# Turns for one pair of blocks, sums before the first layer, and one gate for the gathers of four units

## The chip, the cores and the metric

The kernel runs on one core of a Trainium2 chip. The metric is the device time of one launch in microseconds, the median of three runs. Engines are named as in the profile: PE is TensorE's matmuls, PEld its weight loads, DVE VectorE, ACT ScalarE, POOL GpSimd, SP SyncE.

## The reference, cut to what matters

One layer of a graph network over 6250 nodes of 256 features and 206250 edges, sorted by their target node `dst`:

```
h    = relu(layernorm(x))
e    = relu(raw @ W_e1.T + b_e1) @ W_e2.T + b_e2       # raw: 64 features of an edge
emb  = (e * (clip(edge_attr[:, 0], 0, 1) + 0.01)) @ W_le.T + b_le
msg  = relu(h[src] + emb)
aggr = segment_sum(msg, dst)
g    = (h + aggr) @ W_g1.T + b_g1
out  = x + relu(layernorm(g) * ln_g + ln_b) @ W_g2.T + b_g2
```

All of it is in float32.

## The kernel before, in words

Edges are cut into 403 blocks of 512 and these into 806 units of 256 (two tiles of 128 edges). W_e2 and W_le are multiplied once at the start, so an edge needs a first layer (64 to 256) and one product (256 to 256). Everything is unrolled, and the order on every engine is the order in which the program emits it (a hand-written schedule). The loop runs over units `u`; `now` is the unit in hand. What it emits for a unit:

- `edge_part(u)` (L317): four matmuls (L325, 128x128 weights, 256 columns) into one of seven PSUM banks, which go round in a ring (`BANKS`, class `Ring`); DVE adds the offset and writes `msg[u]` (L331), which frees the bank. In the trace each float32 matmul stands as two records.
- `turn_of(u // 4)`, if `u % 4 == TURN`. A pair `q` is two blocks, that is four units. A turn holds `first_layer(q + 2)` (L278: for each half `c` of the 256 outputs, one matmul for each of the two blocks, each on 64 rows, L292; then ACT and DVE apply bias and relu, L308 and L305, and free the four banks), the segment sums (`add_pairs`, L735, called as `sums`), and the load of the raw features of a later pair on SP's queue (`load_pair`, L273).
- `piece()`: a piece of the 0/1 matrices for the sums (L663, DVE).
- `whole(v)` (L677) for units that lie `lag` units behind: DVE multiplies `msg[v]` by the edge's polarity and adds the gathered row of `h` (L685, in place in `hg[v]`), ACT applies the relu (L690). `lag` falls from 18 to 1 in the course of the kernel, and is one more in the unit ahead of a turn.
- `due()` (L904): a step of the work on 128 finished nodes (two transposes L166 and L199, two products L181 and L212), four steps for each such block of nodes, kept out of the units that `QUIET` names.

The sums of a block (`add_up`, L692) are four matmuls (L703), one for each tile, each with a 0/1 matrix of 32 columns and into its own 32 partitions of the bank `pd`. `add_pairs` takes all pairs whose units `whole` has been through; the first of its matmuls for a pair waits for the newest of these units.

In the middle of the list (`by_two(q)`: 6 <= q < 196) every second turn does the work of two pairs: sums for two pairs, then two first layers, then two loads; the turns between are empty. At both ends each turn does one pair, first layer first.

The rows of `h` are fetched by POOL, two indirect DMAs to a unit (`gather`, L627, issued at L634), into 20 buffers `hg` (`HG`). `got` counts gathers, `summed` the pairs whose sums have been emitted; a gather may run at most 20 units ahead of these. `in_step` (L646), called as `paced` after every unit and after each half of a first layer, adds PE's planned time to `spent` (EDGE 1.754 for a unit, LAYER 0.9 for half a first layer; `add_up` adds SUMS 0.46 a block, `due` NODES 0.81 a step) and emits gathers as long as `(got - 8) * STEP` is below `spent + AFLOAT` (1.288 and 6.0). The first gather that a call emits waits for the matmul that was just emitted; the others follow it on POOL's queue. From unit 782 on, gathers are emitted without such a wait as far as the buffers go.

Of the kernel before, what the change touches and what calls it, by code (L numbers as in the profile page):

```python
# [36 lines left out]
NP = -(-NB // 2)  # L37
# [3 lines left out]
LEAD = 22  # L41
LEAST = 1
EDGE, LAYER, SUMS, NODES = 1.754, 0.9, 0.46, 0.81
STEP = 1.288
AFLOAT = 6.0
BANKS = 7
SHRINK = 44
RAW = 4
HG = 16 + RAW
FEW = 6  # L50
QUIET = (0, 1)
TURN = 1
# [21 lines left out]
def groups_of(w):  # L74
    return [g for g in range(NG) if w in windows_of(g)]
# [25 lines left out]
def gnn_kernel(ctx: ExitStack, tc: tile.TileContext, x, src_c, dst_c, dst_r, pol_c, raw_t, w_e1t, w_e2,  # L101
# [37 lines left out]
    def behind(ins, other):  # L139

        if other is not None:
            tc.add_manual_dep(ins.ins, other.ins.name, mybir.DependencyInfo(
                mybir.DependencyClass.Sync, mybir.DependencyReason.DATA), reason="one wait for several")
# [90 lines left out]
    NU = 2 * NB  # L234
    fast = ExitStack()
    fast.enter_context(tc.manual_schedule())
    with fast:
# [11 lines left out]

        banks = [psz.tile([P, 2, D], F32, name=f"pz{i}") for i in range(BANKS)]  # L250

        class Ring:
# [4 lines left out]
            def __call__(self):  # L257
                self.taken += 1
                return banks[self.taken % BANKS]

# [6 lines left out]
            def old(self):  # L267
                n = self.taken - BANKS
                return self.readers.get(n), self.writers.get(n)
# [3 lines left out]
        def load_pair(q):  # L273
            if q < NP:
                raw[q] = ld.tile([P, 512], F32, name="raw")
                nc.sync.dma_start(out=raw[q], in_=raw_t[q])

        def first_layer(q):  # L278

            bs = [b for b in (2 * q, 2 * q + 1) if b < NB]  # L280
            if not bs:
                return
            for b in bs:
                e1[b] = e1_p.tile([P, 2, 512], F32, name="e1")
            pe, z = {}, {}
            for c in range(2):
                olds = []
                for s, b in enumerate(bs):
                    pe[s, c] = ps().rearrange("p a b -> p (a b)")
                    olds.append(ps.old())  # L290
                for s, b in enumerate(bs):
                    z[c] = nc.tensor.matmul(pe[s, c], we1_s[s * F:(s + 1) * F, c * P:(c + 1) * P],  # L292
                                            raw[q][s * F:(s + 1) * F, :], start=True, stop=True)
                    ps.wrote(z[c], len(bs) - 1 - s)
                    reader, writer = olds[s]
                    if reader is not None and writer is not None:
                        tc.declare_no_dep(z[c].ins, writer.ins, reason="the bank's reader has waited for it")
                    if s == 0:
                        for reader, _ in olds[1:]:
                            behind(z[c], reader)  # L300
                paced(LAYER, z[c])
            for c in range(2):
                for s, b in enumerate(bs):
                    if s == c == 1:
                        a = nc.vector.tensor_scalar(e1[b][:, c, :], pe[s, c], be1_s[:, c:c + 1], 0.0, op0=ALU.add,  # L305
                                                    op1=ALU.max)
                    else:
                        a = nc.scalar.activation(e1[b][:, c, :], pe[s, c], AF.Relu, bias=be1_s[:, c:c + 1])  # L308
                    behind(a, z[c])
                    ps.read(a, len(bs) * (1 - c) + len(bs) - 1 - s)  # L310
            raw.pop(q)
# [23 lines left out]

        last_z = None
        sums = lambda last: None
        paced = lambda us, behind: None

        def by_two(q):  # L340
            return FEW <= q < NP - FEW

        def turn_of(q):


            if not by_two(q):
                if q + 2 < NP:
                    first_layer(q + 2)
                sums(q == NP - 1)
                load_pair(q + 4)  # L350
            elif q % 2 == 0:
                sums(False)
                first_layer(q + 2)
                first_layer(q + 3)
                load_pair(q + 4)
                load_pair(q + 5)

        def forward(u):

            edge_part(u)  # L360
            if u % 4 == TURN:
                turn_of(u // 4)
# [44 lines left out]
        with tc.tile_pool(name="p1", bufs=4) as p1, tc.tile_pool(name="p1x", bufs=11) as p1x:  # L407
# [76 lines left out]
            for k in range(len(parts) + 1):  # L484
# [21 lines left out]
                for _ in range((k > 0) + (k > 2 and k % 3 > 0)):  # L506
                    u = next(units, None)
# [37 lines left out]
        def rows_of_edges():  # L545
            nc.vector.tensor_tensor(
                rel[:, :full].rearrange("p (g k j) -> p g k j", k=L, j=S),
                dst_f[:, :full].rearrange("p (g k j) -> p g k j", k=L, j=S),
                base_b[:, :NF, :].rearrange("p g (o j) -> p g o j", o=1).to_broadcast([P, NF, L, S]), ALU.subtract)
            nc.vector.tensor_tensor(rel[:, full:], dst_f[:, full:], base_b[:, NF, :], ALU.subtract)  # L550
# [63 lines left out]
        with tc.tile_pool(name="hg", bufs=HG - RAW) as hg_p, tc.tile_pool(name="ms", bufs=4) as ms_p, \  # L614
# [5 lines left out]
            got = 2 * RAW  # L620
# [3 lines left out]
            summed = 0  # L624
            spent = 0.0

            def gather(behind=None):  # L627

                nonlocal got
                u, i = divmod(got, 2)  # L630
                got += 1
                if i == 0:
                    hg[u] = (hx_p if u % HG < RAW else hg_p).tile([P, 2, D], F32, name="hg")
                g = nc.gpsimd.indirect_dma_start(  # L634
                    out=hg[u][:, i, :], out_offset=None, in_=hb_d,
                    in_offset=bass.IndirectOffsetOnAxis(ap=src_s[:, 2 * u + i:2 * u + i + 1], axis=0))
                if behind is not None:
                    tc.add_manual_dep(g.ins, behind.ins.name, mybir.DependencyInfo(
                        mybir.DependencyClass.Sync, mybir.DependencyReason.DATA), reason="gathers in step with PE")

            def gathers(last):

                while got < 2 * min(NU, last):
                    gather()

            def in_step(us, behind):  # L646

                nonlocal spent
                spent += us
                while (got - 2 * RAW) * STEP < spent + AFLOAT and got < 2 * min(NU, 4 * summed + HG):  # L650
                    gather(behind)
                    behind = None

            def select(g):

                return [(g, lambda k=k: rows_of_block(g, k)) for k in range(len(blocks_of(g)))]
# [11 lines left out]
            def piece():  # L668

                due_now = [s for s in steps if s[0] <= now][:1]  # L670
                if due_now:
                    steps.remove(due_now[0])
                    due_now[0][1]()
                elif rest:
                    rest.popleft()[1]()
# [81 lines left out]
            now = 0  # L757
# [146 lines left out]
            def due():  # L904

                nonlocal spent
                fns = todo.pop(now, deque())
                if fns and not (by_two(now // 4) and now % 8 in QUIET):
                    spent += NODES
                    fns.popleft()()  # L910
                if fns:
                    todo.setdefault(now + 1, deque()).extendleft(reversed(fns))

            gathers(RAW + 1)
            sums = add_pairs
            paced = in_step
            def strips():
                rows_of_edges()
                rest.extend(select(0) + select(1))
# [4 lines left out]
            now = LEAD  # L924
# [7 lines left out]
            for u in range(LEAD, NU):  # L932
                now = u
                forward(u)

                if u >= NU - 24:
                    gathers(4 * summed + HG)

                piece()
                lag = max(LEAST, LEAD - RAW - u // SHRINK) + (by_two(u // 4) and (u + 1) % 8 == TURN)  # L940
                ready_for = min(u + 1 - lag, 5 * (u + 1 - LEAD) // 4)
                while made < ready_for:
                    gathers(made + 1)
                    whole(made)
                    made += 1
                due()
                for fn in moves.pop(now, []):
                    fn()
                if len(rest) > 6:
                    piece()  # L950
                if u == NU - 24:
                    for w in range(NW):
                        if groups_of(w)[-1] == NG - 1:
                            late[w] = node_work(w, True)
                if u == LEAD + 60:
                    flag = nc.values_load(bad_i[0:1, 0:1], min_val=0, max_val=4 * P)
            while todo:
                now = min(todo)
# [207 lines left out]
```

## Time and profile before

| | |
|---|---|
| median of three runs | 2580.12 us (2579.11 to 2582.3) |
| the profiled execution, its own time | 2579.07 us |
| its span, first to last instruction | 2577.4 us |
| mean granted TensorE clock | 0.946 |
| gathers (POOL, L634) | 1604, 1574.1 us busy |
| edge matmuls (L325) | 6448 records, 1494.5 us busy |
| first layer (L292) | 1612 records, 487.4 us busy |
| segment sums (L703) | 3216 records, 259.2 us busy |

A row of a group reads: line, engine, operation, output<-inputs, shapes, count | busy us, mean ns of one | idle us of the engine just before, and what ended it. A row of the timeline reads: start us, duration us, engine, line, what, count [idle us before <- what ended it]; rows that follow each other without a gap are merged. A row of waits reads: engine, tile, line <- what it waited for: us in total, how often, the longest. A row of windows reads: from:to, length, then busy us and instructions of PE, PEld, DVE, ACT and POOL, the granted clock, the DMA share and GB/s. "issue" is time in which an engine waited for nothing that the profile shows.

### The profile page before, as it was taken

How to read it: one execution, taken by the hardware profiler on the slowest of the kernel's cores; microseconds unless marked ns; L12 is line 12 of the kernel's file. 1: busy time of each engine (PE TensorE's matmuls, PEld its weight loads, DVE VectorE, ACT ScalarE, POOL GpSimd, SP SyncE). 2: the span in 40 equal slices, each digit the busy share in tenths (PEclk: the TensorE clock that was granted, in tenths of full speed). 3: DMA queues.
4: the chain of work that ended last, by engine and by line, in shares of the span. 5: the costliest groups of instructions: out<-in, count | busy, mean ns of one | idle time of the engine just before them, and what ended most of it. 6: DMA issues, size and time to landing. Idle time of an engine off the chain costs nothing.

```text
span 2577.4 us, 36784 instructions
## 1 busy us (share of the span) xinstructions
PE 2314.6 (90%) x11940; PEld 1634.7 (63%) x11940; DVE 1613.4 (63%) x3705; ACT 1019.3 (40%) x1804; POOL 1618.9 (63%) x1675
## 2 busy tenths in 40 slices
PE   9988999989989998988888999998989899888968
PEld 6666666666657666666666666665667566666646
DVE  7866666666656665665656565665656566656636
ACT  7443434343334434343433333343434334333423
POOL 6666666666656666666666666666666666666661
PEclk9899999999989999999999999999999999999989
DMA  9443444434444434443444444444434445443441
GB/s 306 139 135 113 121 123 131 130 115 133 125 118 136 132 112 129 129 132 112 125 125 122 132 134 118 122 130 129 136 115 117 129 123 148 117 132 114 121 119 47
DMA packets 176430, 330.30 MB, mean 128 GB/s; under 512 B 39055, under 2 KB 98280, under 8 KB 176232
## 3 DMA queue, kind: packets, MB, share of 16 engines
q0 software_dynamic: 77376, 211.39, 29.2%
q1 hardware_dynamic: 97556, 113.22, 13.7%
q10 hardware_dynamic: 1300, 3.28, 0.4%
q8 instruction: 95, 1.56, 0.2%
q14 instruction: 103, 0.84, 0.1%
HBM read 293.92 MB, written 33.82 MB: 127 GB/s over the span
## 4 chain that ended last, share of the span: by engine, by line
PE 81%; issue 8%; DVE 5%; another core or an unknown queue 3%; ACT 3%; DMA 0%; ACTq 0%; DVEq 0%
PE pz L325 50%; PE pz L292 17%; PE pd L703 8%; DVE hg L685 2%; PE pz L181 2%; PE pz L212 2%; DVE msg L331 1%; ACT e L308 1%; ACT hg L690 1%; PE pz L166 0%; PE pz L199 0%; DVE st L151 0%; DVE sel L663 0%; ACT xt L440 0%
## 5 line engine op out<-in xcount | busy, mean ns | idle before, releaser
L634 POOL DMA_INDIRECT hg<-hb_d,src_s x1604 | 1574.1, 981 | 897.5 <-issue 520.0
L325 PE MATMUL pz<-wc_s,e 128*128 128x256 f32 x6448 | 1494.5, 388 | 15.5 <-issue 13.0
L325 PEld LDWEIGHTS pz<-wc_s,e 128*128 128x128 f32 x6448 | 1236.4, 194 | 281.6 <-ACT e L308 65.1
L690 ACT ACTIVATE hg<-hg 128x512 f32<-128x512 f32 x805 | 507.5, 630 | 988.5 <-DVE hg L685 800.8
L331 DVE TENSOR_TENSOR msg<-pz,bc_s 128x512 f32<-128x512 f32 x799 | 545.0, 684 | 404.9 <-remote 163.5
L685 DVE SCALAR_TENSOR_TENSOR hg<-msg,pol_s,hg 128x256 f32<-128x256 f32 x1612 | 694.7, 476 | 0.4
L292 PE MATMUL pz<-raw,we_s 64*128 64x512 f32 x1612 | 487.4, 696 | 141.6 <-ACT e L308 86.8
L305 DVE TENSOR_SCALAR e<-pz,vecs 128x512 f32<-128x512 f32 x201 | 150.8, 750 | 504.6 <-PE pz L292 358.4
L308 ACT ACTIVATE e<-pz,vecs 128x512 f32<-128x512 f32 x605 | 367.0, 692 | 202.3 <-PE pz L292 147.9
L292 PEld LDWEIGHTS pz<-raw,we_s 64*128 64x128 f32 x1612 | 177.0, 210 | 395.6 <-issue 232.8
L703 PE MATMUL pd<-hg,sel 128*32 128x256 f32 x3216 | 259.2, 388 | 88.1 <-issue 81.1
L703 PEld LDWEIGHTS pd<-hg,sel 128*32 128x32 f32 x3216 | 110.9, 109 | 216.6 <-issue 163.4
L718 ACT ACTIVATE ms<-pd 128x256 f32<-128x256 f32 x66 | 25.3, 383 | 318.8 <-remote 133.2
L663 DVE SCALAR_TENSOR_TENSOR sel<-iota_w,zero_c,rel 128x128 f32<-128x128 f32 x403 | 137.8, 342 | 0.0
L181 PE MATMUL pz<-wg_s,hT 128*128 128x256 f32 (+1 forms) x196 | 52.8, 393 | 2.6 <-ACT hg L690 2.1
L212 PE MATMUL pz<-wg_s,nT 128*128 128x256 f32 (+1 forms) x196 | 50.8, 382 | 2.0 <-ACT nT L203 1.8
L181 PEld LDWEIGHTS pz<-wg_s,hT 128*128 128x128 f32 (+1 forms) x196 | 37.7, 195 | 10.4 <-ACT hg L690 2.5
L212 PEld LDWEIGHTS pz<-wg_s,nT 128*128 128x128 f32 (+1 forms) x196 | 36.8, 190 | 8.7 <-ACT nT L203 2.7
L444 POOL TENSOR_TENSOR hb<-xt,rows_b 128x256 f32<-128x256 f32 (+1 forms) x49 | 34.1, 728 | 10.5 <-ACT xt L440 4.4
L203 ACT ACTIVATE nT<-pz,vecs 128x128 f32<-128x128 f32 (+1 forms) x98 | 38.7, 444 | 2.6 <-PE pz L199 2.4
L800 DVE TENSOR_TENSOR stb<-stb,ab 128x256 f32<-128x256 f32 x94 | 38.7, 411 | 0.0
L230 DVE SCALAR_TENSOR_TENSOR xt<-xt,zero_c,rows_b 128x128 f32<-128x128 f32 (+1 forms) x98 | 33.5, 343 | 0.0
(108 smaller groups left out, 376.2 us busy)
## 6 DMA issues: line engine op xcount, KB each, us to landing
raw<-in_raw_t_dram SPq DMA_DIRECT2D x202, 256.0 KB
hg<-hb_d,src_s POOLq DMA_INDIRECT x1604
sum_d<-zrow SPq DMA_DIRECT2D x94, 128.0 KB
ab<-sum_d SPq DMA_DIRECT2D x94, 128.0 KB
sum_d<-ms SPq DMA_DIRECT2D x264, 32.0 KB
hb_d<-hb SPq DMA_DIRECT2D x12, 512.0 KB
xt<-in_x_dram SPq DMA_DIRECT2D x48, 128.0 KB
out_dram<-ot SPq DMA_DIRECT2D x48, 128.0 KB
```

The lines of the kernel that those rows point to most:

```text
L181: z = nc.tensor.matmul(ph[:n, 0, :], aT[:, c, :n], wg1_s[:, c, :], start=c == 0 and not bias_by_pe, stop=c == 1)
L212: z = nc.tensor.matmul(po[:n, 0, :], nT[:, c, :n], wg2_s[:, c, :], start=c == 0, stop=c == 1)
L292: z[c] = nc.tensor.matmul(pe[s, c], we1_s[s * F:(s + 1) * F, c * P:(c + 1) * P], raw[q][s * F:(s + 1) * F, :], start=True, stop=True)
L305: a = nc.vector.tensor_scalar(e1[b][:, c, :], pe[s, c], be1_s[:, c:c + 1], 0.0, op0=ALU.add, op1=ALU.max)
L308: a = nc.scalar.activation(e1[b][:, c, :], pe[s, c], AF.Relu, bias=be1_s[:, c:c + 1])
L325: last_z = nc.tensor.matmul(pz[:, i, :], e1[b][:, c, k:k + P], wc_s[:, c, :], start=c == 0, stop=c == 1)
L331: ps.read(nc.vector.tensor_add(msg[u], pz, bc_s))
L634: g = nc.gpsimd.indirect_dma_start(out=hg[u][:, i, :], out_offset=None, in_=hb_d, in_offset=bass.IndirectOffsetOnAxis(ap=src_s[:, 2 * u + ...
L663: nc.vector.scalar_tensor_tensor(sel[g][:, k * S:(k + 1) * S, :], iota_w.rearrange("p (o w) -> p o w", o=1).to_broadcast([P, S, W]), zero_ ...
L685: product = nc.vector.scalar_tensor_tensor(hg[u][:, i, :], m[:, i, :], pol_s[:, 2 * u + i:2 * u + i + 1], hg[u][:, i, :], op0=ALU.mult, op ...
L690: done[u] = product, nc.scalar.activation(hg[u], hg[u], AF.Relu)
L703: z = nc.tensor.matmul(acc[g][j * W:(j + 1) * W, :], sel[g][:, k * S + j, :], m[:, j % 2, :], start=k == 0, stop=b == blocks_of(g)[-1])
```

## The change

In the middle of the list each turn now does one pair: its sums, then one first layer, then one load. At the ends nothing changes in that order. `in_step` still adds to `spent` at every call, but emits gathers only where it is called with `gate`, which is after the first half of a first layer; there it lets the gathers go for one more round (`HALF`: four units, a whole first layer, the sums of two blocks and a node step, 10.546). One such call without a matmul to wait for is made before the loop. The units that `QUIET` keeps free of node work, and the unit in which `lag` is one more, are counted modulo 4 where they were counted modulo 8.

```diff
+HALF = 4 * EDGE + 2 * LAYER + 2 * SUMS + NODES
 ...
                 # first_layer, after the matmuls of half c
-                paced(LAYER, z[c])
+                paced(LAYER, z[c], c == 0)
 ...
         def turn_of(q):
+            if by_two(q):
+                sums(False)
+            if q + 2 < NP:
+                first_layer(q + 2)
             if not by_two(q):
-                if q + 2 < NP:
-                    first_layer(q + 2)
                 sums(q == NP - 1)
-                load_pair(q + 4)
-            elif q % 2 == 0:
-                sums(False)
-                first_layer(q + 2)
-                first_layer(q + 3)
-                load_pair(q + 4)
-                load_pair(q + 5)
+            load_pair(q + 4)
 ...
-            def in_step(us, behind):
+            def in_step(us, behind, gate=False):
                 nonlocal spent
                 spent += us
-                while (got - 2 * RAW) * STEP < spent + AFLOAT and got < 2 * min(NU, 4 * summed + HG):
+                while gate and (got - 2 * RAW) * STEP < spent + AFLOAT + HALF and got < 2 * min(NU, 4 * summed + HG):
                     gather(behind)
                     behind = None
 ...
-                if fns and not (by_two(now // 4) and now % 8 in QUIET):
+                if fns and not (by_two(now // 4) and now % 4 in QUIET):
 ...
             paced = in_step
+            in_step(0.0, None, True)
 ...
-                lag = max(LEAST, LEAD - RAW - u // SHRINK) + (by_two(u // 4) and (u + 1) % 8 == TURN)
+                lag = max(LEAST, LEAD - RAW - u // SHRINK) + (by_two(u // 4) and (u + 1) % 4 == TURN)
```

More of the change, by code (lines that the diff above doesn't have):

```diff
@@ L337, in gnn_kernel @@
         sums = lambda last: None
-        paced = lambda us, behind: None
+        paced = lambda us, behind, gate=False: None
         def by_two(q):
```

## The prediction

> **What bounds the kernel now.** I read the page first, then the groups of instructions between 200 and 2400 us (the steady part), TensorE's (PE's) waits there, and then the timeline around single turns, PE beside GpSimd (POOL). A turn is the place where the edge matmuls (L325) stop for the segment sums (L703) and the first layer (L292).
>
> ```profile
> span 2577.4 us, 36784 instructions
> PE 2314.6 (90%) x11940; PEld 1634.7 (63%) x11940; DVE 1613.4 (63%) x3705; ACT 1019.3 (40%) x1804; POOL 1618.9 (63%) x1675
> PE 81%; issue 8%; DVE 5%; another core or an unknown queue 3%; ACT 3%; DMA 0%; ACTq 0%; DVEq 0%
> ```
> ```profile
> L325 PE MATMUL pz<-wc_s,e 128*128 128x256 f32 x5557 | 1282.7, 387 | 1.6 <-DVE xt L230 0.9 <-issue 0.7
> L634 POOL DMA_INDIRECT hg<-hb_d,src_s x1430 | 1400.5, 979 | 800.9 <-issue 469.4 <-PE pz L325 70.9 <-PE pz L292 58.4
> ```
> ```profile
> PE pd L703 <- issue: 74.1, 105, 1.8
> PE pz L292 <- ACT e L308: 71.5, 32, 5.0
> PE pz L292 <- issue: 44.5, 40, 4.1
> ```
>
> PE sets the end: 81% of the chain. A matmul stands in the trace as two records, so a pair of blocks (four units of four matmuls) has 32 records of L325. 5557 records in 2200 us are 173.7 pairs, **12.67 us for a pair**. The idle time of PE lies at the turns alone: L325 waits for nearly nothing (1.6 us), L703 and L292 for 190 us, most of it under "issue", where nothing that the profile shows was awaited. What that is, the timeline tells. Two-pair turns, the first undisturbed, then three that are not:
>
> ```profile
> 2402.86 1.93 PE L703 MATMUL pd<-hg,sel 128*32 128x256 f32 x32
> 2404.73 3.70 PE L292 MATMUL pz<-raw,we_s 64*128 64x512 f32 x16
> 2408.36 6.96 PE L325 MATMUL pz<-wc_s,e 128*128 128x256 f32 x31
> ...
> 456.40 1.92 PE L703 MATMUL pd<-hg,sel 128*32 128x256 f32 x19
> 459.36 1.09 PE L703 MATMUL pd<-hg,sel 128*32 128x256 f32 x13 [1.04 <-issue]
> ...
> 357.08 2.27 PE L703 MATMUL pd<-hg,sel 128*32 128x256 f32 x30
> 360.39 0.59 PE L703 MATMUL pd<-hg,sel 128*32 128x256 f32 x2 [1.04 <-issue]
> ...
> 560.18 1.91 PE L703 MATMUL pd<-hg,sel 128*32 128x256 f32 x27
> ```
> ```profile
> 2399.52 0.95 POOL L634 DMA_INDIRECT hg<-hb_d,src_s  x1 [0.30 <-issue]
> 2404.06 0.94 POOL L634 DMA_INDIRECT hg<-hb_d,src_s  x1 [3.60 <-issue]
> 446.35 0.94 POOL L634 DMA_INDIRECT hg<-hb_d,src_s  x1 [1.69 <-PE pz L325]
> 456.85 0.95 POOL L634 DMA_INDIRECT hg<-hb_d,src_s  x1 [0.30 <-issue]
> 460.12 1.14 POOL L634 DMA_INDIRECT hg<-hb_d,src_s  x1 [2.33 <-issue]
> 358.32 0.94 POOL L634 DMA_INDIRECT hg<-hb_d,src_s  x1 [0.30 <-issue]
> ```
>
> Gathers come in runs, one right behind the other. At 2402.86 POOL had been quiet since 2400.47: the turn takes 5.50 us to the next L325. At 456.40 a run begun at 446.35 was still on: 19 records went, then PE crept, and went on at 459.36, 1.56 us after the last gather's end (456.85 + 0.95). At 357.08, 30 records went, and the last two came 1.13 us after the run's end. So dense matmuls under a run of gathers use up what PE has in hand (19, 30 and 27 records in the three), and then starve until the run is over. Edge matmuls alone, a third as dense (31 records in 6.96 us against 32 in 1.93), go on under a run. They too starve if a turn has emptied PE and the run goes on:
>
> ```profile
> 2477.30 1.93 PE L703 MATMUL pd<-hg,sel 128*32 128x256 f32 x32
> 2479.16 2.00 PE L325 MATMUL pz<-wc_s,e 128*128 128x256 f32 x7
> 2482.97 0.38 PE L325 MATMUL pz<-wc_s,e 128*128 128x256 f32 x1 [1.81 <-issue]
> ```
> ```profile
> 2474.14 0.94 POOL L634 DMA_INDIRECT hg<-hb_d,src_s  x1 [2.32 <-ACT stb L794]
> 2498.06 0.95 POOL L634 DMA_INDIRECT hg<-hb_d,src_s  x1 [0.30 <-issue]
> 2502.73 0.96 POOL L634 DMA_INDIRECT hg<-hb_d,src_s  x1 [3.72 <-issue]
> ```
> ```profile
> 2486.00:2503.00 17.00, 6.13 (x11) 3.15 (x11) 0.00 (x0) 0.00 (x0) 10.23 (x12) 0.50 0.32 92
> ```
>
> Here 20 gathers stood in a row (2474.14 to 2499.01), and PE did 11 records in 17 us.
>
> **The change part by part.** It holds for pairs 6 to 195, 190 pairs; at both ends of the list turns are single already. A single turn there, first layer ahead of sums, and one step of node work:
>
> ```profile
> 2525.79 1.99 PE L292 MATMUL pz<-raw,we_s 64*128 64x512 f32 x8
> 2527.70 1.07 PE L703 MATMUL pd<-hg,sel 128*32 128x256 f32 x16
> 2528.71 1.99 PE L325 MATMUL pz<-wc_s,e 128*128 128x256 f32 x8
> 1410.43 1.03 PE L181 MATMUL pz<-wg_s,hT 128*128 128x256 f32 x4
> ```
>
> *Twice as many turns.* 2525.79 to 2528.71 is 2.92 us against 5.50 for two pairs: 0.17 us more a pair, 190 times 32 us, if nothing disturbs it. The Trainium skill, TensorEngine Tiling (Array Packing), Key Properties, has the rule that a change of tiling mode drains TensorE, which speaks against this change; the trace bears it out, and puts 32 us on it; the page has no figure that would change the sum.
>
> *The undisturbed period.* Edge matmuls 7.0 (31 records took 6.96), node work 0.65 (two steps like L181's and two of half that length for a block of 128 nodes, a quarter of such a block per pair), turn 2.92: 10.57 us. Now it is 12.67, so 2.1 us a pair is lost today, 4.2 a turn. Lost beside starving is the wait for ACT: two pairs in a row take eight of seven PSUM banks (71.5 us in 32 waits). One pair takes four, so that wait goes. Price: minus 71.5 at most, nothing if the turn would have starved there anyway; the period below is built without it.
>
> *The gathers.* The rule of pacing lets got grow until (got - 8) x 1.288 reaches spent + 6 + 10.55, and a pair adds about 10.5 to spent: 8.16 gathers a gate, eight mostly, sometimes nine. The first waits for the first half of the first layer; behind it on POOL are the other gathers of its batch and nothing else in this stage. Eight take 8 x 0.979 + 7 x 0.30 = 9.95 us; with 0.2 to start, a run is on from the gate to **10.15 us** behind it, nine to 11.4. Those who wait for the gathers are VectorE's products: counted through the emission order, 3.5 to 5.5 units are in hand behind a gate where 0 to 2.5 are now, four are used up before the next, so the least lead hardly changes. The eighth gather starts 9.2 us behind the gate and is wanted about 4.5 units, 11.9 us, behind it. I take nothing for this; if it is short, VectorE stops, and behind it the additions that free the PSUM banks; 1 us a pair would be 190 us.
>
> *Where the next sums meet the run.* Of the undisturbed 10.57, sums and half a first layer are 2.2 (1.0 and 1.2). So the next sums start 8.4 us behind the gate, 1.75 us before the run ends. The burst ahead of the gate is 16 records of sums and 4 of first layer: 20, where PE had 19 to 30 in hand in the three turns above. Three things can follow.
> - Starved ahead of the gate: PE goes on 1.3 us behind the run's end (1.13 and 1.56 above), then 0.3 of sums and 1.2 to the gate: 10.15 + 2.8 = 12.95, with 8.16 gathers 13.2 us.
> - Through: 10.57, but POOL's own 8.16 x 1.28 = 10.45 and 0.2 to start, with some quiet, make it 11.0.
> - Through, but emptied: the next run begins within half a us, where the pauses before the runs shown were 1.69 to 3.72 us, and the edge matmuls starve for the whole of it. Run and recovery 11.45; of the 39 records behind the gate some 16 are done meanwhile (ten at once, then 11 in 17 us as in that row), 23 are left (5.0); sums and half layer 2.2: 18.6 us.
>
> One row of the three falls short of 20: I take a third for the first; of the rest, which no row splits, a half through and a sixth emptied: 4.4 + 5.5 + 3.1 = **13.0 us a pair**. The unknown is the split; its ends are all through (11.0 to 11.65) and every second one emptied (14.8).
>
> *The rest.* One raw load a turn on SP's queue instead of two in two, used two turns later as before (about 25 us): nothing; the cover is that lead. Node steps keep out of two units of four instead of two of eight; 0.93 steps a pair have two places: nothing on PE, later only. VectorE puts off one unit's products before each turn, now twice as often; it is busy 63%, 8.0 of 12.67 us a pair, and waits at each turn for the first layer; at 13.0 us it has room, at 11.0 little.
>
> Sum: 190 x (13.0 - 12.67) = +63 us on the profiled execution's 2579.07 (span 2577.4 and 1.7 around it; the median of the runs is 2580.12, 1 us more): **2642 us**.
>
> The Trainium skill, TensorE: Matmul & The Clock Gate, its table of goals, says that PE idle for more than about 3 us falls to half rate. The 0.50 of granted clock in the 17 us row agrees; by it an emptied period would cost another 1 to 2 us, and the sum some 40 us more.
>
> **Rivals.**
> 1. *The burst slips through* (faster). Half as many records per burst, most of it at the end of a run, and no eighth bank. For it: 27 and 30 records in hand in two of three rows. Against: pauses of half a us, and a demand of POOL (10.45) as long as PE's period. The period is then POOL's 10.45, 0.2 and a pause of 1 us, 11.65: 2579 - 190 x 1.02 = 2385 us.
> 2. *Emptied every other time* (much slower). For it: the row of 17 us; batches of nine that run past the gate. Against: PE paused less than that nowhere in the middle. 14.8 us a pair at full weight, 2980; at half of that excess 2780.
> 3. *A trade* (no change): the period stays set by run plus recovery, 10.45 + 2.2 as now; 2579 us. That the gathers are not let go as said is no rival: the gate is in the emission order.
>
> **How the numbers follow.** Forecast 0.46, first rival 0.30, second 0.19, third 0.05. Forecast and second rival make 0.65 for slower, the first rival 0.30 for faster, the third 0.05 for neither; a measurement of this kernel can tell 0.2%, about 5 us. The range reaches from the upper half of the first rival to the middle of the second, 2430 to 2840; about 0.12 is left out below and 0.08 above. Within the forecast alone it would be 2600 to 2720.
>
> **What would show it.** Right: runs of eight gathers begin some 0.2 us behind half a first layer, last 10 us, and end within 2 us behind the next sums' start; L703 split in half or more of the turns with "issue" before the rest; "L292 <- ACT e L308" nearly gone; L325 showing issue waits that it hasn't now (1.6 us). Wrong: sums unbroken at 1.07 us and a period under 12 us; or the new waits being VectorE's for gathers.

## The result, and the profile after

The changed kernel took 2635.2 us (median of four runs, 2631.0 to 2646.53) beside 2579.61 us of the kernel before (2576.83 to 2582.3), measured along with it: a ratio of 1.0234, 95% interval 1.0209 to 1.0259. It is slower, by 55.6 us; 2642 was forecast. The profiled execution took 2646.53 us, 67.5 more than the one before.

Later runs fell on four chips. On three of them before is faster by about a sixth, 2136 to 2149 us, and so is the change on the one of the three where it ran itself. So each experiment below is compared with runs of before on its own chip, and I call a place *stalling* (before 2567 to 2582 us) or *quiet* (2136 to 2149).

First the profile after, in the stalling place: of the page, of the groups between 200 and 2400 us, and of TensorE's (PE's) waits there.

```profile
span 2644.8 us, 35524 instructions
PE 2359.9 (89%) x11940; PEld 1583.1 (60%) x11940; DVE 1599.8 (60%) x3705; ACT 1023.9 (39%) x1804; POOL 1628.8 (62%) x1675
PE 83%; issue 8%; DVE 4%; another core or an unknown queue 3%; ACT 1%; DMA 1%; SPq 0%; DVEq 0%; ACTq 0%
```
```profile
L326 PE MATMUL pz<-wc_s,e 128*128 128x256 f32 x5392 | 1274.5, 386 | 89.9 <-issue 75.3 <-ACT e L309 13.2
L293 PE MATMUL pz<-raw,we_s 64*128 64x512 f32 x1344 | 388.0, 682 | 4.6 <-issue 3.6
L699 PE MATMUL pd<-hg,sel 128*32 128x256 f32 x2760 | 274.9, 423 | 134.8 <-issue 103.5 <-ACT hg L686 26.6
L630 POOL DMA_INDIRECT hg<-hb_d,src_s x1389 | 1369.6, 986 | 832.6 <-issue 557.4 <-PE pz L293 151.8 <-PE pz L326 24.6
```
```profile
PE pd L699 <- issue: 103.5, 107, 6.3
PE pz L326 <- issue: 75.3, 92, 2.5
PE pd L699 <- ACT hg L686: 26.6, 12, 5.5
```

(Edge matmuls are now L326, the first layer L293, the sums L699, the gathers L630.) 5392 records of L326 in 2200 us are 168.5 pairs, **13.06 us a pair** against 12.67. The wait of the first layer for ScalarE, 71.5 us before, is gone. In its place edge matmuls wait 89.9 us where they waited 1.6, most of it "issue", and the sums 134.8 where they waited 81.0. One turn that passes and the next that starves, PE beside GpSimd (POOL):

```profile
1311.78 3.40 PE L326 MATMUL pz<-wc_s,e 128*128 128x256 f32 x15
1315.11 1.07 PE L699 MATMUL pd<-hg,sel 128*32 128x256 f32 x16
1316.11 1.99 PE L293 MATMUL pz<-raw,we_s 64*128 64x512 f32 x8
...
1323.12 3.62 PE L326 MATMUL pz<-wc_s,e 128*128 128x256 f32 x16
1327.05 0.66 PE L699 MATMUL pd<-hg,sel 128*32 128x256 f32 x4 [0.31 <-issue]
1328.48 1.09 PE L699 MATMUL pd<-hg,sel 128*32 128x256 f32 x3 [0.77 <-issue]
...
1336.59 3.78 PE L293 MATMUL pz<-raw,we_s 64*128 64x512 f32 x8
```
```profile
1311.33 0.94 POOL L630 DMA_INDIRECT hg<-hb_d,src_s  x1 [2.63 <-issue]
1322.06 0.94 POOL L630 DMA_INDIRECT hg<-hb_d,src_s  x1 [0.82 <-issue]
1332.50 0.95 POOL L630 DMA_INDIRECT hg<-hb_d,src_s  x1 [0.30 <-issue]
1338.95 0.95 POOL L630 DMA_INDIRECT hg<-hb_d,src_s  x1 [5.49 <-PE pz L293]
```

The run of gathers begun at 1311.33 was still on when the gate at 1317 was passed, so the next batch followed 0.82 us behind it: 17 gathers in a row, to 1333.45. PE got through a whole turn and the next edge matmuls, then starved in the sums from 1327 until after the run's end. Of the 189 turns, counted in the trace from the start of the sums to the end of the first layer, 138 passed in 2.99 us (under 3.1), 18 took 3.1 to 6 and 33 took 6 to 13.7.

### The profile page after: what moved, and what is told of

Its sections match the earlier page's. It is cut to its first block, busy times and chain, and to the rows that moved or that the text cites. A ratio compares the mean times of both kernels' runs of the same rounds, so it can differ in the third digit from the quotient of the medians.

```text
span 2644.8 us, 35524 instructions
## 1 busy us (share of the span) xinstructions
PE 2359.9 (89%) x11940; PEld 1583.1 (60%) x11940; DVE 1599.8 (60%) x3705; ACT 1023.9 (39%) x1804; POOL 1628.8 (62%) x1675
## 4 chain that ended last, share of the span: by engine, by line
PE 83%; issue 8%; DVE 4%; another core or an unknown queue 3%; ACT 1%; DMA 1%; SPq 0%; DVEq 0%; ACTq 0%
PE pz L326 51%; PE pz L293 16%; PE pd L699 11%; DVE hg L681 2%; PE pz L213 2%; PE pz L182 2%; DVE msg L332 1%; ACT e L309 1%; PE pz L200 1%; DVE sel L659 0%; DMA raw<-in_raw_t_dram 0%; ACT hg L686 0%; PE pz L167 0%; DVE e L306 0%
## 5 line engine op out<-in xcount | busy, mean ns | idle before, releaser
L630 POOL DMA_INDIRECT hg<-hb_d,src_s x1604 | 1583.9, 987 | 955.6 <-issue 625.4
L326 PE MATMUL pz<-wc_s,e 128*128 128x256 f32 x6448 | 1522.1, 386 | 105.0 <-issue 85.1
L326 PEld LDWEIGHTS pz<-wc_s,e 128*128 128x128 f32 x6448 | 1207.4, 191 | 453.4 <-issue 215.4
L309 ACT ACTIVATE e<-pz,vecs 128x512 f32<-128x512 f32 x605 | 377.1, 685 | 544.8 <-PE pz L293 180.5
L293 PE MATMUL pz<-raw,we_s 64*128 64x512 f32 x1612 | 468.3, 682 | 24.0 <-DVE msg L332 13.4
L699 PE MATMUL pd<-hg,sel 128*32 128x256 f32 x3216 | 313.4, 421 | 144.2 <-issue 112.0
L293 PEld LDWEIGHTS pz<-raw,we_s 64*128 64x128 f32 x1612 | 160.6, 208 | 244.7 <-issue 205.8
L699 PEld LDWEIGHTS pd<-hg,sel 128*32 128x32 f32 x3216 | 105.5, 114 | 323.5 <-issue 250.9
```

Of the source, the lines that this page charges most:

```text
L326: last_z = nc.tensor.matmul(pz[:, i, :], e1[b][:, c, k:k + P], wc_s[:, c, :], start=c == 0, stop=c == 1)
L630: g = nc.gpsimd.indirect_dma_start(out=hg[u][:, i, :], out_offset=None, in_=hb_d, in_offset=bass.IndirectOffsetOnAxis(ap=src_s[:, 2 * u + ...
L699: z = nc.tensor.matmul(acc[g][j * W:(j + 1) * W, :], sel[g][:, k * S + j, :], m[:, j % 2, :], start=k == 0, stop=b == blocks_of(g)[-1])
```

## The experiments

Theory 1 is the prediction's: PE starves under runs of gathers. Rivals: the price of twice as many turns (theory 2), and rows that come late or the traffic of the rows, rather than POOL's work (theory 3).

**The turns without the gate.** The change, paced as before (the one call ahead of the loop goes too):

```diff
-                while gate and (got - 2 * RAW) * STEP < spent + AFLOAT + HALF and got < 2 * min(NU, 4 * summed + HG):
+                while (got - 2 * RAW) * STEP < spent + AFLOAT and got < 2 * min(NU, 4 * summed + HG):
```

> The turns of the change with the pacing of before (gathers emitted after every unit and every half of a first layer). Theory 1 (on record: TensorE starves where its sums fall into a run of gathers on GpSimd): bursts of 20 records instead of 40 and no wait for an eighth bank, with short runs of gathers between, so faster than before: 2400 to 2530 us, few sums split. Theory 2 (twice as many turns are what costs): as slow as the change, 2600 to 2680 us, with clean turns.

2160.43 us beside 2140.74: ratio 1.0095 [1.0078, 1.0112], in a quiet place, below both ranges. No turn was stalled, so theory 1 could not show; what did show is a net price of the turns, about 20 us.

**The gate without the turns.** Before, with one gate for eight units (`HALF` doubled):

```diff
-                paced(LAYER, z[c])
+                paced(LAYER, z[c], c == 0 and q % 2 == 0)
```

> The turns of before for two pairs, with one gate for the gathers of eight units after the first half of the first of the two first layers. Theory 1: runs of 16 gathers last 20 us of a period of about 21, so the next 32 records of sums start within the run and starve in most turns: 2650 to 2900 us. Theory 2 (turns, not the gate): like before, 2560 to 2600 us.

2138.92 us, 0.9993 [0.9983, 1.0002], same place. The gate alone costs nothing there; neither range came, since nothing stalled.

**Plain loads in place of the gathers.** The change, twice, on two quiet chips:

```diff
-                g = nc.gpsimd.indirect_dma_start(
-                    out=hg[u][:, i, :], out_offset=None, in_=hb_d,
-                    in_offset=bass.IndirectOffsetOnAxis(ap=src_s[:, 2 * u + i:2 * u + i + 1], axis=0))
+                r = (got * 97) % (N - P)
+                g = nc.sync.dma_start(out=hg[u][:, i, :], in_=hb_d[r:r + P, :])
```

> The change with each gather replaced by a plain load of 128 rows from the same table, issued on SyncE's queue at the same place and behind the same matmul. The rows are not those of the edges: the gather itself is left out. Theory 1 (GpSimd's work on the gathers holds TensorE up): no starving, a period near the undisturbed 10.57 us, 2180 to 2300 us. Theory 3 (the traffic of the rows, or rows that land late, hold TensorE up): the same bytes at the same time, 2580 to 2680 us.

> The change with plain loads on SyncE's queue in place of GpSimd's gathers (the gather left out), once more. Where before takes about 2580: 2150 to 2200 us if GpSimd's work on the gathers is what stalls TensorE, 2580 to 2680 if it is the traffic of the rows or a slow TensorE as such. Where before takes about 2140: 2160 us by both, which tells nothing apart.

2160.24 and 2161.72 us (one run each), as with gathers (2161.45 below) and under both ranges of the first expectation. In a quiet place the gathers cost the changed kernel nothing. What stalls PE in the other place this doesn't tell: it was never run there.

**Sums of a constant tile.**

```diff
-                    z = nc.tensor.matmul(acc[g][j * W:(j + 1) * W, :], sel[g][:, k * S + j, :], m[:, j % 2, :],
+                    z = nc.tensor.matmul(acc[g][j * W:(j + 1) * W, :], sel[g][:, k * S + j, :], wc_s[:, j % 2, :],
```

> The change with the segment sums reading a constant tile in place of the finished rows, so what is summed is left out; number, shape and order of the matmuls stay, and the first of a pair still waits for the newest unit. Theory 1 (records are used up, whatever they read): unchanged, 2600 to 2690 us, as many split sums. Theory 3 (the split sums wait for rows that come late): sums no longer split, 2250 to 2450 us.

2161.78 us (one run), quiet place: there are no stalls for it to remove, and neither range came. It tells nothing on theory 3.

**The change once more.**

> The changed kernel itself once more. The kernel before took 2140.74 us in the first experiments where it took 2579.61 when it was first measured, and the turns alone took 2160.43 with no stalled matmul. If the stalls under runs of gathers belong to the place where a kernel runs (theory 1a), then where before takes about 2140 the change takes 2155 to 2165 with clean turns, and where before takes about 2580 it takes 2630 to 2650. If they belong to the gate (theory 1b), the change takes over 2250 us even where before takes 2140.

2161.45 us beside 2140.99: 1.0095 [1.0076, 1.0113], on another quiet chip. This fits theory 1a: the stalls belong to the place. Its page, its groups between 200 and 2000 us and one turn:

```profile
span 2158.7 us, 35524 instructions
PE 2142.4 (99%) x11940; PEld 1534.3 (71%) x11940; DVE 1602.2 (74%) x3705; ACT 1027.4 (48%) x1804; POOL 1629.5 (75%) x1675
```
```profile
L630 POOL DMA_INDIRECT hg<-hb_d,src_s x1395 | 1374.9, 986 | 425.0 <-issue 325.1 <-DMA hg<-hb_d,src_s 31.4 <-ACT hg L686 22.9
L326 PE MATMUL pz<-wc_s,e 128*128 128x256 f32 x5443 | 1248.8, 382 | 0.0
L293 PE MATMUL pz<-raw,we_s 64*128 64x512 f32 x1360 | 337.9, 615 | 0.0
L699 PE MATMUL pd<-hg,sel 128*32 128x256 f32 x2784 | 185.5, 385 | 0.0
```
```profile
1208.91 1.07 PE L699 MATMUL pd<-hg,sel 128*32 128x256 f32 x16
1209.91 1.99 PE L293 MATMUL pz<-raw,we_s 64*128 64x512 f32 x8
1211.83 2.00 PE L326 MATMUL pz<-wc_s,e 128*128 128x256 f32 x8
```

PE waits for nothing in 1800 us, and POOL's row says that it was never idle but for 0.3 us between two gathers (1374.9 + 425.0 = 1799.9; 425.0 / 1395 = 0.305): one unbroken run of 1395 gathers, with every burst of sums inside it, and no burst broken. So a run of gathers doesn't by itself starve PE. 5443 records are 10.58 us a pair.

**Before once more, and before with plain loads** (the edit as above), on a third quiet chip.

> The kernel before, for a profile of it in the condition in which it takes about 2140 us. If the first profile's lost time (2.1 us a pair) was stalls under gathers that this condition lacks, PE is busy 97% of the span or more, L703 is never split, and turns for two pairs take 5.50 to 5.57 us but for waits for a PSUM bank of some 20 us in all. If the gathers still cost something, issue waits at L703 stay over 50 us.

> The kernel before with each gather replaced by a plain load of 128 rows of the same table on SyncE's queue, issued at the same place (the gather itself is left out). Where before takes about 2140: 2130 to 2145 if gathers cost TensorE nothing there; under 2125 if part of the 2140 is still theirs. Where before takes about 2580: 2130 to 2200 if GpSimd's gathers are what stalls TensorE, about 2580 if a slow TensorE or the traffic is.

2142.11 and 2112.56 us (one run each). The groups of before between 200 and 2000 us, a turn of it, and the edge matmuls of the kernel with plain loads:

```profile
L634 POOL DMA_INDIRECT hg<-hb_d,src_s x1408 | 1371.3, 974 | 429.2 <-issue 316.1 <-PE pz L325 26.5 <-DMA hg<-hb_d,src_s 24.7
L325 PE MATMUL pz<-wc_s,e 128*128 128x256 f32 x5506 | 1240.2, 381 | 0.0
L685 DVE SCALAR_TENSOR_TENSOR hg<-msg,pol_s,hg 128x256 f32<-128x256 f32 x1409 | 637.1, 480 | 271.1 <-DMA hg<-hb_d,src_s 267.1 <-DVE sel L663 0.3
L292 PE MATMUL pz<-raw,we_s 64*128 64x512 f32 x1376 | 324.7, 606 | 11.3 <-ACT e L308 6.1 <-DVE msg L331 5.1
```
```profile
1207.21 1.93 PE L703 MATMUL pd<-hg,sel 128*32 128x256 f32 x32
1209.07 3.70 PE L292 MATMUL pz<-raw,we_s 64*128 64x512 f32 x16
1212.71 1.99 PE L325 MATMUL pz<-wc_s,e 128*128 128x256 f32 x8
```
```profile
L325 PE MATMUL pz<-wc_s,e 128*128 128x256 f32 x5568 | 1253.7, 381 | 0.0
```

Here POOL holds before back: again it makes no pause (1371.3 + 429.2 = 1800.5), and VectorE waits 267.1 us for rows, which it doesn't in the change. PE is busy 98% of the span and waits 18 us in this stretch, none of it "issue", as was expected; the sums too were held up four times, 6.8 us in all, by ScalarE. Period 10.46 us (5506 records). With plain loads it is 10.34 (5568) and the kernel 29.6 us faster. So in a quiet place the gathers cost before some 30 us and the change nothing.

**Sums of two pairs, first layers one by one.** The change, with

```diff
-            if by_two(q):
+            if by_two(q) and q % 2 == 0:
                 sums(False)
```

> The change with the sums of two pairs in every second turn and none between, first layers one to a turn as in the change. Where before takes about 2140 and the change 2161: if each unbroken stretch of one kind of matmul has a fixed price (sums 0.13 us: 16 records take 1.00 and 32 take 1.87 from start to start; first layer 0.20 us; edges 0.13), 95 stretches of sums fewer save 12 us: 2149. If all of the price hangs on the sums' 32-column tiles, about 2140 or less; if on the first layer and the edges alone, 2161.

2152.57 us, 1.0055 [1.0035, 1.0074]. Against the change's 1.0095 that is 0.4%, 8.6 us, where a fixed price for each stretch of sums said 12. So part of the price goes with the number of stretches of sums; not all of it hangs on their 32-column tiles.

**Turns taken apart.** Sums of one block after the first and third unit of a pair, half a first layer after the second and fourth, gathers paced as before the change (the lines that carry it):

```diff
+            if by_two(q):
+                if r == 1:
+                    some_sums(0)
+                elif r == 2:
+                    half_layer(q + 2, 0)
+                elif r == 3:
+                    some_sums(1)
...
+            if r == 0 and by_two(q - 1):
+                half_layer(q + 1, 1)
+                load_pair(q + 3)
```

> Single turns taken apart: sums of one block after the first and the third unit of a pair, half a first layer after the second and the fourth, gathers emitted after every unit as before; four short bursts of 8 and 4 records in place of one of 24. Theory 1 (TensorE starves when a dense burst uses up its records under a run of gathers): where before takes about 2580, 2250 to 2450 us. Theory 2 (each change between edge matmuls, sums and first layer has a price, about 0.2 us a pair for the change's turns): four places of change in a pair in place of one add 0.4 to 0.8 us a pair, so where before takes 2140, 2230 to 2310 us.

2329.83 us, 1.0882 [1.0862, 1.0902]: 168 us over the change in the same place, 0.89 us a pair, a little more than the 0.4 to 0.8 of theory 2. (The pacing is no part of it: the turns without the gate took 2160.43.) The timeline of PE:

```profile
1199.82 1.99 PE L361 MATMUL pz<-wc_s,e 128*128 128x256 f32 x8
1201.74 1.13 PE L328 MATMUL pz<-raw,we_s 64*128 64x512 f32 x4
1202.80 1.99 PE L361 MATMUL pz<-wc_s,e 128*128 128x256 f32 x8
1204.73 0.64 PE L747 MATMUL pd<-hg,sel 128*32 128x256 f32 x8
1205.30 0.44 PE L200 MATMUL pz<-ident,hs 128*128 128x128 f32 x2
```

From start to start: edges 1.92 a stretch, half a first layer 1.06, sums of a block 0.57. Nothing waits; the matmuls are the same, only in shorter stretches.

**Gathers without pacing.** The kernel before, first with the gathers let go as far as the buffers allow, then also with six units in place of four gathered from `x` ahead of the table:

```diff
-                while (got - 2 * RAW) * STEP < spent + AFLOAT and got < 2 * min(NU, 4 * summed + HG):
-                    gather(behind)
-                    behind = None
+                while got < 2 * min(NU, 4 * summed + HG):
+                    gather()
```
```diff
-RAW = 4
-HG = 16 + RAW
+RAW = 6
+HG = 20
...
-        with tc.tile_pool(name="p1", bufs=4) as p1, tc.tile_pool(name="p1x", bufs=11) as p1x:
+        with tc.tile_pool(name="p1", bufs=4) as p1, tc.tile_pool(name="p1x", bufs=10) as p1x:
```

> The kernel before with gathers let go as far as the buffers allow, none waiting for a matmul. Where before takes about 2140: if GpSimd's row of gathers sets its end (1604 of 1.28 us from 63.9 us on), only its early pauses (2.46 us and some short ones) are to be had: 2134 to 2139. If the waits for matmuls hold gathers back in the middle, 2110 to 2125. Where before takes about 2580: runs without pauses stall the sums in nearly every turn, over 2650.

> The same, and six units in place of four gathered from x itself before the table is done (four gathers fewer behind it; one buffer less for the first loads of x, to make room). Where before takes about 2140: the row of gathers is four times 1.28 us shorter behind the table, 5 us off free: 2129 to 2134, if the table isn't done later. If the row of gathers doesn't set the end, as free.

These fell on a chip where before took 2576.27 us: 3265.2, ratio 1.2643 [1.2599, 1.2687], and 3252.34, ratio 1.2629 [1.2607, 1.2652]. Of the second: page, groups between 200 and 2900 us, and PE beside POOL in one run.

```profile
PE 2493.3 (77%) x11940; PEld 1712.1 (53%) x11940; DVE 1605.9 (49%) x3715; ACT 1028.7 (32%) x1808; POOL 1595.2 (49%) x1675
PE 61%; issue 16%; DVE 10%; another core or an unknown queue 9%; ACT 2%; DMA 1%; SPq 0%; ACTq 0%; DVEq 0%
```
```profile
L325 PE MATMUL pz<-wc_s,e 128*128 128x256 f32 x5333 | 1461.9, 422 | 371.8 <-issue 344.1 <-ACT e L308 15.9 <-ACT hg L689 3.1
L634 POOL DMA_INDIRECT hg<-hb_d,src_s x1365 | 1314.0, 963 | 1386.5 <-issue 841.4 <-ACT hg L689 408.2 <-ACT stb L793 48.7
```
```profile
1227.80 1.99 PE L292 MATMUL pz<-raw,we_s 64*128 64x512 f32 x8
...
1237.70 7.07 PE L325 MATMUL pz<-wc_s,e 128*128 128x256 f32 x31
1246.52 0.38 PE L325 MATMUL pz<-wc_s,e 128*128 128x256 f32 x1 [1.75 <-issue]
1248.62 2.44 PE L212 MATMUL pz<-wg_s,nT 128*128 128x256 f32 x4 [1.73 <-issue]
```
```profile
1227.28 0.95 POOL L634 DMA_INDIRECT hg<-hb_d,src_s  x1 [9.22 <-ACT hg L689]
1246.47 0.94 POOL L634 DMA_INDIRECT hg<-hb_d,src_s  x1 [0.30 <-issue]
1258.99 1.08 POOL L634 DMA_INDIRECT hg<-hb_d,src_s  x1 [11.58 <-ACT hg L689]
```

Gathers now come sixteen in a row (1227.28 to 1247.41), then POOL waits for buffers, and the issue share of the chain doubles from 8% to 16%. 5333 records in 2700 us are 16.2 us a pair. This bears theory 1 out for a stalling place: the same program, only with longer runs, takes a quarter more. PE's "issue" waits are 452 us in these 2700 us, where before has 120 in 2200; another 186 us are waits for ScalarE and VectorE, so not all of the loss is shown to be stalls under gathers. Counted in the traces (a pause of over 0.9 us parts two runs), 96 of 96 runs of sixteen or more have a gap over 0.55 us between two starts of PE, and so have all 34 runs of fifteen or more in the changed kernel there, but only 33 of its 125 runs of seven to nine. That the same kernel without pacing is harmless in a quiet place wasn't tried; that before and the change run gathers without a pause there is in the rows above.

No version beat before: the gate alone equals it in a quiet place, and the 2112.56 us of before with plain loads is no version, since the rows aren't those of the edges.

## Why the prediction was right, and where it was not

*The undisturbed period* of 10.57 us was 10.58 wherever nothing stalled. *The price of single turns* was measured again exactly: 1208.91 to 1211.83 is 2.92 us, 1207.21 to 1212.71 is 5.50 for two, 0.17 us a pair. But it isn't the whole price. Change and before, both with plain loads, differ by 48 us (2160.24 and 2161.72 against 2112.56, one run each and on three chips), of which 32 lie in the turns; the rest lies outside, where edge matmuls too are cut into shorter stretches: 10.58 - 2.92 = 7.66 us of edges and node work a pair against 10.34 - 2.75 = 7.59, some 13 us over 190 pairs. That term was sized too small by a third. The Trainium skill, TensorEngine Tiling (Array Packing), Key Properties, has a drain at each change of tiling mode. The turns taken apart agree (168 us more with nothing waiting).

*The wait for ScalarE* went, as said. *The batches* came as said: 125 of 160 runs are of seven to nine gathers (counted in the trace, as above). *The stalls*: the prediction had 2.43 us a pair (13.0 - 10.57) where two-pair turns had 2.27 (12.67 - 10.40). With the undisturbed periods now measured it is 13.06 - 10.58 = 2.48 against 12.67 - 10.34 = 2.33. So by this difference, which takes the quiet places' periods for the stalling one too, the loss by stalls hardly grew, 0.15 us a pair or 29 us, and the price of the turns, 0.24 us or 45 us, is the larger part of the 0.39. The two sum to 74 us on the profiles' middle, where the executions differ by 67.5.

*Records in hand* is the step that failed, by its size. I read 19 to 30 from the bursts alone. But PE had worked under the same run before each burst: counted from the run's start, the three rows of the prediction give 65, 77 and 74 records ahead of the first pause. In the starved turn above it was some 80 (the 55 shown, 2 of a transpose at 1311.4 and 22 in the lines left out), and in the unpaced kernel the gap came 17 us into the run (1227.28 to 1244.77). Counted in the traces, with PE starved where it idles over 0.25 us on "issue", half of the first pauses came behind 50 to 63 records of a run in before, 56 to 81 in the change and 52 to 66 without pacing. In time that is 7.4 to 9.3 us behind the run's start in before and 10.2 to 15.2 in the change, so the count fits the kernels better than the time. In the change the runs that PE survived had 56 records (the median), and only 3 of 113 had 70 or more. So what decides, as far as these counts tell, is whether PE comes to some 50 to 80 records before POOL pauses: a run of eight mostly ends in time, two merged ones don't (34 of 34). Why it is that many stays open.

*The split* drawn from it failed too: a third starved ahead of the gate, a half through, a sixth emptied were forecast; 73% went through (138 of 189), and the loss sits in the others (257 us over 2.99 each, summed from the trace, most of it where two batches had merged) and in the edge matmuls behind them. Merging stands where the prediction had emptied. It was about as rare as said (34 of 160 runs), but it carries most of the loss, and PE does not starve from the gate on, as said: in the turn shown it got through the edge matmuls and starved in the next sums. In all, the sums wait 103.5 us on "issue" and the edge matmuls 75.3. That the mean came out at 13.06 for 13.0 is therefore partly luck: a wrong split with about the right sum. "L703 split in half or more of the turns" was wrong: 31 of 189 had a pause over 0.3 us in the sums.

*The condition* was not seen at all. The forecast took the stalls for a property of the kernel. On three other chips before doesn't stall, nor does the change on the one where it ran, and there the balance is another one: the turns' price of 48 us, less the 30 us that before lost to POOL's rate and the change does not, about 20 us (1.0095). That 30 goes with VectorE's wait for rows in before; in the change it is nothing there, as I took it. The sign held there, by the turns' price, which was half of the forecast's 63 us.

*The clock.* The prediction's sentence on it speaks of a pause of about 3 us. In the stretch of 17 us at 0.50 the longest pause of PE was 1.86 us (ahead of 2486.55), so here the clock fell without one.

*Open*: what makes a place stall. POOL's work on the gathers and the traffic of the rows could only be told apart by plain loads in a stalling place. Gathers took the same time in both (986 ns in the change's two profiles). The Trainium skill, Runtime: NRT & Kernel Launch, Instruction fetch mechanics, has each engine's instructions come in blocks of 16 KiB by a DMA queue of its own; a row of the profile agrees in size,

```profile
q8 instruction: 94, 1.54, 0.2%
```

and such packets would be a candidate for "issue" waits, but in the trace of the change the stalled time is spread from some 6 to 30 us behind the last packet, and the packets took 0.88 to 1.84 us there and 0.88 to 1.81 in the quiet place, so a late block alone doesn't explain it.

## What to carry to other kernels

Before a stall is designed around, find out whether it is the kernel's: time the same program in another place, and look whether the same overlap goes unpunished there. A turn that changes the kind of matmul has a fixed price that shows in the stretches on both sides of it, so cost it from the periods of two kernels that nothing else bounds, not from the turn alone. When an engine shows idle stretches of one fixed length (0.3 us between gathers) and no other, it is full, whatever its busy share says.

## What the runs showed of the hardware that was not expected

- One program took 2580 us in one place and 2141 on three other chips; the change 2635 and, on the one of the three where it ran, 2161. The granted clock was 0.946 and 0.931 in the first, 0.993 to 0.999 on the others. The low clock goes with the stalls (0.854 in the unpaced kernel with 344 us of issue waits of edge matmuls alone): in the stalling place an undisturbed turn of before had 1.00 (the row below, third from its end), and the stretch of 20 gathers in the prediction 0.50. What the low clock adds to the loss was not measured.

```profile
2402.00:2409.00 7.00, 7.00 (x56) 3.46 (x55) 3.43 (x6) 2.80 (x5) 3.78 (x4) 1.00 0.54 168
```

- POOL at 75% busy was POOL full: 0.974 us a gather and 0.305 us between two (never under 0.303 in these 1800 us), 1.28 us in all, 10.2 us for the eight of a pair against 10.34 that PE needs at best.
- Where PE stalls under gathers, it first gets through some 50 to 80 records counted from the run's start, and the loss grows with the run's length: without pacing the kernel takes 26% longer there.
